# Head of a two-FFN transformer block: order by hand, tile by tile; rows without a slot made beside the experts; the sort moved behind the routing

## The chip, the cores and the metric

The kernel runs on one core of one Trainium2 chip. The metric is the device time of one execution in microseconds. Three runs of the kernel before took 4994.91 us (median), 4991.19 and 4998.73 us; a profiled execution, from which all rows below come, took 4992.54 us.

## The reference

Input x is 8 x 1024 tokens of 512 float32 values, T = 8192 tokens in all. Three steps follow one another, each on a layer norm LN without gain or offset:

```
x = x + 0.5 * FFN(LN(x));   x = x + Attention(LN(x));   x = x + 0.5 * FFN(LN(x))

FFN(h), E = 32 experts, C = 320 slots each, F = 512:
  probs = softmax(h @ w_router); top1 = argmax; gate = probs[top1]
  pos = place of the token among those of its expert, in token order
  accepted = pos < C
  y = (silu(g) * u) @ w_down,  g = h @ w_gate[top1],  u = h @ w_up[top1]
  return h + where(accepted, gate * y, 0)
```

The FFN returns h plus the expert's part, so each step adds x + h/2 to every token, and gate * y / 2 to those that got a slot. A token beyond the 320th of its expert has no slot and keeps x + h/2 alone. Attention has 16 heads of 32 and rotary tables. The same weights serve both FFNs.

## The kernel before

The work runs in four stages on one core: the head (routing for the first FFN), the first experts, the attention (which also routes for the second FFN), and the second experts.

**Head** (`tile_macaron`, L1215 to L1245). Eight groups of G = 8 tiles of 128 tokens. Each group is loaded in one DMA of 2 MB (L1231). Per tile, DVE takes mean and variance (`stats`, L113 and L114); per group, `normalizing` makes the scale: DVE adds epsilon (L124), POOL takes the power -0.5 (L125), DVE makes the shift `nmr` (L127) and the pair r2, n2 (L128, L129) for x + h/2. ACT writes h (`normalize`, L134), DVE writes x + h/2 in place (`rest`, L148), and the whole group goes to the DRAM array x1 (L1238). Per four tiles `logits` transposes h on PE (`tp`, L156), copies it on ACT (`xT`, L157), multiplies by the router (`pl`, L177), copies (`parts`, L182), folds (`lp`, L187) and copies (`lg`, L190). Per group `route` (L216 to L265) makes softmax and slots: mx, ex (exp on ACT, L219), one-hot `oh`, running counts `run`, two products on PE (`pp`, L234 and L238), position, and at last the integer `slot` (L265). Then POOL issues one indirect DMA per tile (L267), which writes each token's number and gate into the table at its slot. In this stage the framework's scheduler chooses the order of instructions.

**Experts** (`experts`, called once for each FFN). First the table is read back (`slots`, L378, on SP), DVE clears the two buffers `a` (L382), and `sorted` ranks the experts by their counts (L280 to L340), with its products in PSUM; DVE then copies part of the slots (L384), two products permute the slots (`pt`, L387), and POOL gathers the first experts' tokens (L454). SP loads each expert's three matrices (1 MB each, L445) as soon as the sorted `order` is there. `arm`, also from the sort, picks one of three code versions by the counts. The loop `feed` then runs 32 experts: products for gate and up (`gp`, `up`, L511), Silu on ACT (`sg`, L516), product on DVE (`a`, L534), transposes of the next expert (L499), down projection (`yp`, L547), the sum with x + h/2 (`ys`, L551), and one indirect DMA per 128 tokens (L565), which writes the finished rows. So in the first FFN the experts overwrite the rows of x1 of all tokens with a slot. Order on PE, ACT, DVE and POOL is as written; SP's queue is placed by the scheduler.

**Attention** (`Attention.run`) reads x1, works through heads by an order written out by hand, and in its last part routes for the second FFN in groups of four tiles (`finished`). Its end copies the counts, and `experts` starts again.

DMAs issued from SP go through one hardware queue in order; indirect DMAs are issued by POOL, one after another, in line with POOL's other instructions.

Of the kernel before, what the change touches and what calls it, by code (L numbers as in the profile page):

```python
# [22 lines left out]
P = 128  # L23
# [27 lines left out]
class Block:  # L51
# [64 lines left out]
    def normalizing(self, pool, mv):  # L116

        nc, G = self.nc, mv.shape[1]  # L120
        r, n, r2, n2 = (
            pool.tile([P, G], F32, tag=name, name=name) for name in ("rstd", "nmr", "r2", "n2")
        )
        nc.vector.tensor_scalar(r, mv[:, :, 1], EPS, None, ALU.add)  # L124
        nc.gpsimd.tensor_tensor(r, r, self.power[:, 0:G], ALU.pow)  # L125
        yield WAIT, 2
        nc.vector.scalar_tensor_tensor(n, mv[:, :, 0], -1.0, r, ALU.mult, ALU.mult)  # L127
        nc.vector.tensor_scalar(r2, r, 0.5, 1.0, ALU.mult, ALU.add)  # L128
        nc.vector.tensor_scalar(n2, n, 0.5, None, ALU.mult)  # L129
        return r, n, r2, n2  # L130
# [21 lines left out]
    def transposed(self, psum, tag, out, x):  # L152

        tp = psum.tile([P, self.KD, P], F32, tag=tag, name="tp")
        for k in range(self.KD):
            self.nc.tensor.transpose(tp[:, k, :], x[:, k * P : (k + 1) * P], self.ident)  # L156
        self.copy(out, tp)  # L157

    def logits(self, hs, lg, pool, psum, tag, bufs=2):

        nc, E, KD = self.nc, self.E, self.KD
        xT = pool.tile([P, KD, 4 * P], F32, tag="xT", bufs=bufs, name="xT")
        j = 0
        for h in hs:
            if isinstance(h, tuple):
                yield h
                continue
            yield PE, 0.6  # L170
            self.transposed(psum, tag, xT[:, :, j * P : (j + 1) * P], h)
            j += 1
        yield WAIT, 1
# [7 lines left out]
        parts = pool.tile([P, 4 * P], F32, tag="parts", bufs=1, name="parts")  # L181
# [11 lines left out]
    def route(self, t0, lg, pool, psum, tag, carry, table):  # L193
# [71 lines left out]
        nc.vector.tensor_scalar(slot, s, float(self.NS), None, ALU.add)  # L265
        for j in range(G):
            nc.gpsimd.indirect_dma_start(  # L267
                out=table[t0 + j],
                out_offset=bass.IndirectOffsetOnAxis(ap=slot[:, j : j + 1], axis=0),
                in_=row[:, j, :],  # L270
                in_offset=None,
            )
        return run[:, G, :]

    def sorted(self, pool, psum, counts, order, arm):
# [9 lines left out]
        pc = psum.tile([P, E], F32, tag="tp", name="pc")  # L285
        nc.tensor.matmul(pc, self.ones, counts, start=True, stop=True)
        pr = psum.tile([R, P], F32, tag="tp", name="pr")
# [3 lines left out]

        keys, mine = pool.tile([P, E], F32, name="keys"), pool.tile([R, E], F32, name="mine")
        nc.vector.scalar_tensor_tensor(keys, pc, float(E), self.rev[:, 0, :], ALU.mult, ALU.add)
        nc.vector.tensor_scalar(mine, pr[:, 0:E], float(E), None, ALU.mult)
# [26 lines left out]
        nc.vector.tensor_copy(cols[:, 1, :], pr[0:E, :])  # L321
        over, some = pool.tile([P, E], F32, name="over"), pool.tile([P, 2], F32, name="some")
        for i in range(2):
            pq = psum.tile([P, E], F32, tag="tp", name="pq")
# [15 lines left out]
        return matrix  # L340

    def experts(self, table, counts, src, dst, w_gate, w_up, w_down):
# [9 lines left out]
        views = dram_disjoint_views(dst, E * NB)  # L352
# [3 lines left out]
        with tc.tile_pool(name="et", bufs=1) as tp:  # L356
            R = NB * E
            order, come, go = (tp.tile([P, w], I32, name=name) for name, w in
                               (("order", E), ("come", R), ("go", R)))
            at = [tp.tile([P, R], F32, name=f"at{i}") for i in range(2)]  # L360
            ids, gates = at
            arm = tp.tile([P, 1], I32, name="arm")
# [9 lines left out]
            with (  # L372
# [8 lines left out]
                for t in acts:  # L381
                    nc.vector.memset(t, 0.0)  # L382
                matrix = self.sorted(fp, ps, counts, order, arm)
# [25 lines left out]
            for i in tc.Switch(which, len(self.profiles)):  # L409
                with (  # L410
# [5 lines left out]
                    expert = Expert(self, (wp, ap, ps), src, views, come, go, gates, acts)  # L416
# [10 lines left out]
class Expert:  # L427


    def __init__(self, s, pools, src, views, come, go, gates, acts):  # L430
        self.s, self.nc = s, s.nc
        self.wp, self.ap, self.ps = pools
        self.src, self.views = src, views
        self.come, self.go, self.gates, self.acts = come, go, gates, acts

        self.xs = 3 if self.wp is not self.ap else 2
# [11 lines left out]
    def gather(self, r, width):  # L448
# [11 lines left out]
        return SimpleNamespace(r=r, width=width, NB=NB, x=x)  # L460

# [57 lines left out]
    def feed(self, now, following, after):  # L519
# [5 lines left out]
        a, wd = self.acts[now.r % 2], now.weights[2]  # L525
        if following:
            self.measure(following)
        later = after and after()
        for f in range(KF):
# [5 lines left out]
            if following and f == 1:  # L535
                self.rests(following)
        if following:
# [34 lines left out]
class Attention:  # L572
# [13 lines left out]
    def __init__(  # L586
        self, s, L, B, x1, x2, out, table, inverse, zero, counts, weights, biases, cos, sin
# [3 lines left out]
        self.x1, self.x2, self.out, self.table, self.carry = x1, x2, out, table, zero  # L591
        self.inverse, self.counts = inverse, counts
# [121 lines left out]
    def run(self):  # L714
        nc, tc = self.nc, self.tc
        F, KD = mybir.EngineType, self.KD
        with (
# [6 lines left out]
            with tc.manual_schedule(engines={F.PE, F.Activation, F.DVE, F.Pool}):  # L724
# [29 lines left out]
                nc.vector.tensor_copy(self.counts, self.carry)  # L754
# [430 lines left out]
def tile_macaron(  # L1185
# [11 lines left out]
    x1 = dram.tile([T, D], F32, name="x1")  # L1197
# [9 lines left out]
    counts = const.tile([P, E], F32, name="counts")  # L1207
# [4 lines left out]

    with (
        tc.tile_pool(name="a", bufs=3) as pool,
        tc.tile_pool(name="aps", bufs=6, space=PSUM) as psum,  # L1215
    ):
        none = pool.tile([P, s.NS // P, 2], F32, tag="none", bufs=1, name="none")
        nc.vector.memset(none[:, :, 0], float(T))
        nc.vector.memset(none[:, :, 1], 0.0)
# [4 lines left out]
        views = dram_disjoint_views(tables[0], NT)  # L1224
        carry = zero
        for g in range(NG):
            rows = slice(g * G * P, (g + 1) * G * P)
            xg = pool.tile([P, G, D], F32, tag="xg", name="xg")
            hg = pool.tile([P, G, D], F32, tag="hg", name="hg")
            mv = pool.tile([P, G, 2], F32, tag="mv", name="mv")  # L1230
            nc.sync.dma_start(xg, xf[rows, :].rearrange("(j p) d -> p j d", p=P))  # L1231
            for j in range(G):
                s.stats(pool, mv[:, j, :], xg[:, j, :])
            by = at_once(s.normalizing(pool, mv))
            for j in range(G):
                s.normalize(hg[:, j, :], xg[:, j, :], by, j)
                s.rest(xg[:, j, :], xg[:, j, :], by, j)
            nc.sync.dma_start(x1[rows, :].rearrange("(j p) d -> p j d", p=P), xg)  # L1238
            lg = pool.tile([P, G, E], F32, tag="lg", name="lg")
            for j in range(0, G, 4):  # L1240
                at_once(s.logits(
                    [hg[:, j + i, :] for i in range(4)], lg[:, j : j + 4, :], pool, psum, "ps"
                ))
            carry = at_once(s.route(g * G, lg, pool, psum, "ps", carry, views))
        nc.vector.tensor_copy(counts, carry)  # L1245

    s.experts(tables[0], counts, xf, x1, w_gate, w_up, w_down)


    Attention(  # L1250
        s, L, B, x1, x2, of, dram_disjoint_views(tables[1], NT), inverse, zero, counts,
        (wqT, wkT, wvT, woT), (bq, bk, bv, bo), cos, sin,
    ).run()

    s.experts(tables[1], counts, x2, of, w_gate, w_up, w_down)
# [41 lines left out]
```

## Time and profile before

| Stage | us of the span |
|---|---|
| profiled execution (its own time) | 4992.54 |
| span of its instructions | 4990.8 |
| head: to the last slot | 197.2 |
| last table scatter issued (L267) | 206.37 |
| first product of the first expert (L511) | 240.53 |
| end of the last scatter of the first experts | 1055.5 |
| table read before the second experts (L378) | 4143.46 |
| first product of the second experts | 4174.70 |

A profile row reads: start, duration, engine, line, operation, out<-in, shapes, count, and in brackets the idle time of that engine before it with what ended it. PEld is PE's weight load. "issue" is time in which the engine waited for nothing that the profile shows. Of the span, PE is busy 4661.9 us (93%), DVE 2875.7, ACT 2887.6, POOL 723.8; DMA moves 485.93 MB. PEclk is the granted clock of PE as a share of full speed. Between 50 and 200 us it is 0.71 to 0.73; from 250 us on it is 1.00.

### The profile page before, as it was taken

To read this page: it belongs to the slowest core of one execution; us is meant where nothing else is said; L and a number is where in the kernel's file an instruction comes from. 1 tells how busy PE (TensorE), PEld (TensorE's weight loads), DVE (VectorE), ACT (ScalarE), POOL (GpSimd) and SP (SyncE) were. 2 spreads that over 40 slices of the span, in tenths; PEclk is the share of its full clock that TensorE was granted. 3 is DMA by queue.
4 is the path that set the end of the run, shared out by engine and by line. 5 is a ranking of instruction groups with operands and counts; after the bars stand their busy time and mean duration, and the time that the engine had idled before them with its cause. 6 is when DMAs were issued, how large, how long until landed. Compare 5 with 4: busy or idle time off the path is not lost.

```text
span 4990.8 us, 68660 instructions
## 1 busy us (share of the span) xinstructions
PE 4661.9 (93%) x24568; PEld 2144.3 (43%) x24568; DVE 2875.7 (58%) x5685; ACT 2887.6 (58%) x5794; POOL 723.8 (15%) x702
## 2 busy tenths in 40 slices
PE   4499999978899999999999999999999876999999
PEld 3366667742223333333333333333333224666677
DVE  6433333336766767777777777767766734333333
ACT  5311111107999888888888888888888831111111
POOL 2422222210000010110010110110110002222221
PEclk7699999988999999999999999999999987999999
DMA  6334445531111211212212212212211114445454
GB/s 226 138 126 165 161 167 175 197 110 28 43 27 40 80 50 54 72 46 61 68 45 64 69 41 66 69 41 64 60 42 58 52 65 147 153 162 170 161 194 137
DMA packets 284903, 485.93 MB, mean 97 GB/s; under 512 B 42248, under 2 KB 77522, under 8 KB 284544
## 3 DMA queue, kind: packets, MB, share of 16 engines
q1 hardware_dynamic: 254816, 404.35, 25.3%
q0 software_dynamic: 29440, 76.83, 4.9%
q8 instruction: 196, 3.21, 0.3%
q14 instruction: 163, 1.34, 0.1%
q10 hardware_dynamic: 288, 0.20, 0.0%
HBM read 363.34 MB, written 89.72 MB: 91 GB/s over the span
## 4 chain that ended last, share of the span: by engine, by line
PE 81%; DVE 8%; ACT 4%; issue 3%; POOL 1%; DMA 1%; SPq 1%; DVEq 0%; another core or an unknown queue 0%; ACTq 0%; POOLq 0%
PE sa L1022 13%; PE gp L511 9%; PE up L511 9%; PE pq L927 9%; PE po L1104 8%; PE yp L547 8%; PE sb L1002 5%; PE px L1130 4%; PE pv L972 4%; PE sb L1029 3%; ACT junk L1041 2%; DVE nm L1037 2%; PE tp L156 2%; PE tp L499 2%; PE yp L555 1%
## 5 line engine op out<-in xcount | busy, mean ns | idle before, releaser
L1037 DVE TENSOR_REDUCE nm<-sa 128x2 f32<-128x1024 f32 x1024 | 1249.2, 1221 | 649.9 <-PE sa L1022 391.6
L1041 ACT ACTIVATE junk<-sa,nm 128x512 f32<-128x512 f32 x2048 | 1408.2, 688 | 267.9 <-DVE nm L1037 195.2
L1022 PE MATMUL sa<-k,q 32*128 32x512 f32 x4096 | 1151.4, 646 | 19.6 <-ACT junk L1041 11.5
L1034 ACT ACTIVATE pr<-sb 128x1024 f32<-128x1024 f32 x1024 | 1041.4, 1019 | 101.6 <-PE sb L1029 95.5
L1029 PE MATMUL sb<-q,k 32*128 32x512 f32 x4096 | 1064.3, 603 | 0.0
L516 ACT ACTIVATE sg<-gp 128x320 f32<-128x320 f32 (+3 forms) x256 | 102.9, 402 | 1273.0 <-PE gp L511 973.0
L1104 PE MATMUL po<-pr,v 128*32 128x512 f32 x4096 | 550.1, 608 | 0.1
L511 PE MATMUL gp<-bT,wg 128*128 128x320 f32 (+3 forms) x2048 | 532.9, 403 | 2.6 <-DVE bT L502 2.6
L511 PE MATMUL up<-bT,wu 128*128 128x320 f32 (+3 forms) x2048 | 525.4, 399 | 0.0
L952 POOL TENSOR_TENSOR raw<-raw,cs 128x512 f32<-128x512 f32 x128 | 164.9, 1288 | 2471.9 <-DMA rot<-raw 1880.3
L927 PE MATMUL pq<-hT,wqk 128*128 128x512 f32 x1024 | 511.4, 624 | 7.3 <-DVE raw L942 3.7
L547 PE MATMUL yp<-wd,a 128*128 128x512 f32 x1024 | 453.7, 596 | 0.0
L511 PEld LDWEIGHTS gp<-bT,wg 128*128 128x128 f32 x2048 | 387.7, 191 | 118.7 <-issue 31.4
L1002 PE MATMUL sb<-mrow,ones 3*128 3x512 bf16 x2048 | 393.5, 385 | 45.0 <-ACT pr L1034 42.3
L534 DVE TENSOR_TENSOR a<-sg,up 128x320 f32<-128x320 f32 (+3 forms) x256 | 114.1, 446 | 548.6 <-PE up L511 531.6
L511 PEld LDWEIGHTS up<-bT,wu 128*128 128x128 f32 x2048 | 389.4, 190 | 94.6 <-issue 0.8
L1002 PEld LDWEIGHTS <-ones 3*128 3x128 bf16 x2048 | 100.6, 91 | 714.1 <-issue 672.4
L1041 ACT ACTIVATION_READ_ACCUMULATOR junk<-sa,nm 128x1 f32 x2048 | 397.9, 194 | 0.0
L1029 PEld LDWEIGHTS sb<-q,k 32*128 32x128 f32 x4096 | 360.4, 184 | 0.1
L1022 PEld LDWEIGHTS sa<-k,q 32*128 32x128 f32 x4096 | 305.2, 184 | 84.7 <-ACT pr L1034 34.5
L927 PEld LDWEIGHTS pq<-hT,wqk 128*128 128x128 f32 x1024 | 176.3, 191 | 326.0 <-issue 227.5
L551 DVE SCALAR_TENSOR_TENSOR ys<-yp,at,x 128x512 f32<-128x512 f32 x128 | 96.1, 750 | 369.0 <-PE yp L547 369.0
(175 smaller groups left out, 4213.1 us busy)
## 6 DMA issues: line engine op xcount, KB each, us to landing
wg<-in_w_gate SPq DMA_DIRECT2D x64, 1024.0 KB
wu<-in_w_up SPq DMA_DIRECT2D x64, 1024.0 KB
wd<-in_w_down SPq DMA_DIRECT2D x64, 1024.0 KB
rot<-raw SPq DMA_DIRECT2D x1024, 32.0 KB
xg<-in_x SPq DMA_DIRECT2D x8, 2048.0 KB
x<-xg SPq DMA_DIRECT2D x8, 2048.0 KB
xt<-x SPq DMA_DIRECT2D x64, 256.0 KB
xr<-x SPq DMA_DIRECT2D x64, 256.0 KB
```

The lines of the kernel that those rows point to most:

```text
L511: nc.tensor.matmul(acc, w[:, k, f * P : (f + 1) * P], to.bT[:, k, 0:width], start=(k == 0), stop=(k == s.KD - 1),)
L547: nc.tensor.matmul(yp, a[:, f, i * P : (i + 1) * P], wd[:, f, :], start=(f == 0), stop=(f == KF - 1),)
L927: nc.tensor.matmul(acc, w[:, which, k, :], self.hT[b, n][:, k, :], start=(k == 0), stop=(k == KD - 1),)
L972: nc.tensor.matmul(acc, hT[:, k, at : at + P], self.w_vo[:, k, :], start=(k == 0), stop=(k == KD - 1),)
L1002: nc.tensor.matmul(sb[:, h, :], self.ones16[at : at + 3, :], row[at : at + 3, :], start=True, stop=False,)
L1022: nc.tensor.matmul(sa[:, h, :], qa[at, (g * 4 + j) * P : (g * 4 + j + 1) * P], ka[at, m * 512 : (m + 1) * 512], start=True, stop=True,)
L1029: nc.tensor.matmul(sb[:, h, :], k[at, t * P : (t + 1) * P], q[at, n * 512 : (n + 1) * 512], start=False, stop=True,)
L1034: nc.scalar.activation(pr, sb, AF.Exp)
L1037: nc.vector.tensor_reduce(nm[:, m, j, pair : pair + 2], sa, AX.X, ALU.max, negate=True)
L1041: nc.scalar.activation(self.junk, sa[:, h - pair, :], AF.Exp, bias=nm[:, m, j, h : h + 1], accum_out=se[:, m, j, h : h + 1],)
L1104: nc.tensor.matmul(self.po[at : at + HD, :], self.v[b][t][:, c * P + at : c * P + at + HD], prs[h // 2 * 2][:, h % 2, :], start=(t == 0), ...
L1130: nc.tensor.matmul(acc, self.oT[b, c, half][:, j * P : (j + 1) * P], self.w_vo[:, c, :], start=False, stop=(c == KD - 1),)
```

## The change

Four things are done.

1. The head is written out by hand (`front`) for PE, ACT, DVE and POOL. It goes tile by tile: in each step, h of one tile on ACT, its transposes on PE, the copy of the tile before (seven of eight on ACT, every eighth on DVE), the stats of the tile ten ahead on DVE, and one step of each piece of other work at hand: a group's scale, the router products of four tiles, a route. Groups are 4, then seven times 8, then 4 tiles. Loads are 1 MB (four tiles).
2. x + h/2 isn't made in the head any more, and x1 isn't written there. The scale and shift of all tokens stay in SBUF (`rest`), and `route` also makes `spare`: for a token without a slot its own number, else T.
3. In the first experts' loop, expert r loads two tiles of x, ACT makes x + h/2 of them, and POOL scatters them by `spare`; rows whose index is T fall outside the bounds and are skipped. x1 becomes a DRAM tensor of its own name.
4. `sorted` runs right behind the routing, at the end of the head and at the end of the attention, in a pool of its own; the result is handed to `experts`. The buffers `a` are cleared by POOL.

```diff
-    def normalizing(self, pool, mv):
+    def normalizing(self, pool, mv, to=None):
...
-        r, n, r2, n2 = (
+        r, n, r2, n2 = to or (
...
+        if spare is not None:
+            nc.vector.tensor_scalar(ok, pos, float(C), None, ALU.is_ge)
+            nc.vector.scalar_tensor_tensor(u, token, float(-self.T), ok, ALU.add, ALU.mult)
+            nc.vector.tensor_scalar(spare[:, t0 : t0 + G], u, float(self.T), None, ALU.add)
         for j in range(G):
             nc.gpsimd.indirect_dma_start(
...
+    def front(self, pool, psum, x, rest, spare, carry, table):
...
+        def routed(g):
+
+            while state.next < g:
+                yield
+            state.carry = yield from self.route(
+                starts[g], lgs[g], pool, psum, "lp", state.carry, table, spare
+            )
+            state.next += 1
+
+        def products(t):
+            g = group[t]
+            lg, at = lgs[g], t // 4 * 4 - starts[g]
+            yield from self.routers(
+                xTs.pop(t // 4), lg[:, at : at + 4, :], pool, psum, "lp", bufs=2
+            )
+            if t + 1 == starts[g] + sizes[g]:
+                work.append(routed(g))
...
+        ahead, late = G + 2, None
+        load(0)
+        load(4)
+        for i in range(-ahead, NT + 2):
+            if 0 <= i < NT:
+                g = group[i]
+                if i == starts[g]:
+                    lgs[g] = pool.tile([P, sizes[g], E], F32, tag="lg", bufs=3, name="lg")
+                h = pool.tile([P, D], F32, tag="h", bufs=4, name="h")
+                self.normalize(h, tile_of(i), (r, n, None, None), i)
+                if i % 4 == 0:
+                    xTs[i // 4] = pool.tile([P, KD, 4 * P], F32, tag="xT", bufs=3, name="xT")
+                tp = self.turned(psum, "tp", h)
+            if late:
+                to, from_, j = late
+                (nc.vector.tensor_copy if j % G == G - 1 else nc.scalar.copy)(to, from_)
+                if j % 4 == 3:
+                    work.append(products(j))
+            late = None
+            if 0 <= i < NT:
+                late = xTs[i // 4][:, :, i % 4 * P : (i % 4 + 1) * P], tp, i
+            t = i + ahead
+            if t < NT:
+                if t % 4 == 0 and t + G < NT:
+                    load(t + G)
+                self.stats(pool, mv[:, t, :], tile_of(t))
+                if t + 1 == starts[group[t]] + sizes[group[t]]:
+                    work.insert(0, scaled(group[t]))
+            advance()
+        while work:
+            advance()
+        return state.carry
...
-        pr = psum.tile([R, P], F32, tag="tp", name="pr")
+        nc.vector.scalar_tensor_tensor(keys, pc, float(E), self.rev[:, 0, :], ALU.mult, ALU.add)
+        pr = psum.tile([R, P], F32, tag=tag, name="pr")
...
+        nc.vector.tensor_copy(many, pr)
+        nc.vector.tensor_scalar(mine, many[:, 0:E], float(E), None, ALU.mult)
...
                 for t in acts:
-                    nc.vector.memset(t, 0.0)
-                matrix = self.sorted(fp, ps, counts, order, arm)
+                    nc.gpsimd.memset(t, 0.0)
...
+    def fetch_others(self, r):
+
+        s = self.s
+        n = s.NT // s.E
+        x = self.ap.tile([P, n, s.D], F32, tag="all", name="all")
+        self.nc.sync.dma_start(
+            x, self.src[r * n * P : (r + 1) * n * P, :].rearrange("(j p) d -> p j d", p=P)
+        )
+        return x
+
+    def put_others(self, r, x):
+
+        s, (scale, shift, spare) = self.s, self.others
+        n = s.NT // s.E
+        for j in range(n):
+            t = r * n + j
+            self.nc.scalar.activation(
+                x[:, j, :], x[:, j, :], AF.Identity, bias=shift[:, t : t + 1],
+                scale=scale[:, t : t + 1],
+            )
+            self.nc.gpsimd.indirect_dma_start(
+                out=self.views[s.E * s.NB + t],
+                out_offset=bass.IndirectOffsetOnAxis(ap=spare[:, t : t + 1], axis=0),
+                in_=x[:, j, :], in_offset=None, bounds_check=s.T - 1, oob_is_err=False,
+            )
...
         a, wd = self.acts[now.r % 2], now.weights[2]
+        others = self.fetch_others(now.r) if self.others else None
         if following:
             self.measure(following)
...
+        if others:
+            self.put_others(now.r, others)
         if following:
             self.transpose(following)
...
-                nc.vector.tensor_copy(self.counts, self.carry)
+                self.ranks = self.s.sorted(self.ranking, psum, "m", self.carry)
...
-        for g in range(NG):
...
-            for j in range(G):
-                s.normalize(hg[:, j, :], xg[:, j, :], by, j)
-                s.rest(xg[:, j, :], xg[:, j, :], by, j)
-            nc.sync.dma_start(x1[rows, :].rearrange("(j p) d -> p j d", p=P), xg)
...
+        counts = s.front(
+            pool, psum, xf, rest, spare, zero, dram_disjoint_views(tables[0], NT)
+        )
+        ranks = s.sorted(ranking, psum, "lp", counts)
```

A generator advances by one `yield` in each step of the loop, whatever the yield says: in the head the kinds and sizes that `normalizing`, `routers` and `route` yield are not weighed.

## The prediction

> **What bounds the kernel now.** I read the page first (the slices), then the busy time by stretches, the timeline of the head, and the chain of waits from 160 to 262 us. Line numbers are those of the profile.
>
> ```profile
> span 4990.8 us, 68660 instructions
> PE   4499999978899999999999999999999876999999
> DVE  6433333336766767777777777767766734333333
> POOL 2422222210000010110010110110110002222221
> PEclk7699999988999999999999999999999987999999
> ```
>
> PE is full from the third slice on; only the first two slices (the head) and the two dips near slices 9 and 33 are not PE's. The change touches the head, the first expert loop and the second dip.
>
> ```profile
> 50.00:100.00 50.00, 28.19 (x151) 19.88 (x152) 34.65 (x137) 23.57 (x44) 19.00 (x18) 0.72 0.73 213
> 240.50:300.00 59.50, 59.35 (x212) 36.49 (x214) 20.20 (x49) 9.12 (x15) 11.84 (x13) 0.95 0.37 130
> ```
>
> Columns: stretch, then busy us of PE, PE loads, DVE, ACT, POOL, then granted clock, DMA share, GB/s. In the head no engine is full: engines wait for one another. From 240.5 on PE has 59.35 of 59.5, so there the rest is hidden. The head's waits show best here:
>
> ```profile
> 54.40 0.15 DVE L265 TENSOR_SCALAR slot<-s 128x8 int32<-128x8 f32 x1
> 54.86 1.17 POOL L267 DMA_INDIRECT table<-row,slot  x1 [16.19 <-DVE slot L265]
> ...
> 63.92 0.96 POOL L267 DMA_INDIRECT table<-row,slot  x1 [0.30 <-issue]
> 64.91 1.67 POOL L125 TENSOR_TENSOR rstd<-rstd,power 128x8 f32<-128x8 f32 x1
> 66.61 0.17 DVE L127 SCALAR_TENSOR_TENSOR nmr<-mv,rstd 128x8 f32<-128x8 f32 x1 [5.74 <-POOL rstd L125]
> ...
> 66.82 0.81 ACT L134 ACTIVATE hg<-xg,nmr,rstd 128x512 f32<-128x512 f32 x1 [7.91 <-DVE nmr L127]
> ```
>
> POOL gives out eight scatters one by one, 1.265 us apart, and the power that the next group's scale needs stands behind them: DVE idles 5.74 us, ACT 7.91. This befell two of the eight groups (scatters at 54.86 and 101.60); elsewhere the power ran before the scatters or found POOL free.
>
> ```profile
> 206.37 0.96 POOL L267 DMA_INDIRECT table<-row,slot  x1 [0.30 <-issue]
> 208.73 0.34 SPq L378 DMA_DIRECT2D slots<-table  x1
> 209.18 1.12 DVE L382 MEMSET a<- 128x1280 f32 x1 [11.94 <-DMA table<-row,slot]
> 219.13 0.22 DVE L384 COPY slots<-slots 32x128 f32<-32x128 f32 x1
> 222.13 0.98 POOL L454 DMA_INDIRECT x<-in_x,come  x1 [14.80 <-DVE go L395]
> 240.53 4.60 PE L511 MATMUL gp<-bT,wg 128*128 128x320 f32 x8 [1.41 <-DVE bT L502]
> ```
>
> The way out of the head: last scatter, table read back, two memsets and the sort on DVE (209.18 to 219.13), gather, first expert. The same before the second experts:
>
> ```profile
> 4143.46 0.33 SPq L378 DMA_DIRECT2D slots<-table  x1
> ...
> 4153.45 0.22 DVE L384 COPY slots<-slots 32x128 f32<-32x128 f32 x1
> ```
>
> **The second experts' start.** The sort is moved behind the routing and the memsets to POOL; the read of the table no longer finds the sort in front. Sort: 4145.89 to 4153.42, 7.5 us, plus 0.2 for the added copy and about 1 for its products sharing one PSUM buffer; it starts at 4136.3 behind the slots and ends near 4145. The read, issued at 4143.46, has no landing of its own in the trace: between 1.65 us (`rot<-raw`, 1110.13) and 4.36 (`bias`, 1056.63 to its reader at 1060.99, on a busy queue); I take 2.1, as the scatters land (206.37, 2.09). So the copy of the slots runs at 4145.6 in place of 4153.45: **-7.5 us**, between -5.5 and -8. What hides the sort is four scatters and their landing (4136.61 to 4142.89) and the read; without that cover 7.5 come back. The memsets on POOL cost, by its 128x128 one of 0.208 and 128x1 of 0.10, from 1.2 (slope) to 2.1 us (in proportion) each, so POOL is free by 4147.1 at the latest and the gather is due at 4148.5. SP loads weights about 8 us earlier, but as long before the gather as now (4 us), so the two collide as today.
>
> **The head.** Gone: 64 `rest` operations of DVE (34.9 us) and 16.8 MB of writes. They lie on today's chain in part (`xg` L148 is 2.4% of the chain up to 600 us, 14 us), but the new order makes a chain of its own, so I walk that; the changed kernel as built shows it on each in-order queue. Per eight tiles, DVE: slot, spare, stats, rstd+eps, stats, **nmr**, then one route interleaved with six stats, slot. POOL: eight scatters, then the power for that nmr. ACT: per tile h and the copy of the tile before; two `parts`, two `lg`, one exp. PE: transposes, `pl`, `lp`, `pp` in line with them.
>
> I time it from one group's slot to the next (a cycle).
>
> *Slot to nmr.* The scatters are released at slot and the power comes right behind them: 54.55 (end of slot) to 66.61 = **12.0 us** in the row above; in its place DVE has 2.4 us of work (0.6 spare, two stats at 0.81 as at 358.37 to 359.99, rstd 0.2). Queued behind nmr on DVE are the stats, the next route and every eighth copy of `xT`; ACT stops at the exp that needs this route's `ex`, and PE then runs out of tiles. So all three are late, not DVE alone. Groups 4 to 7 meet it in full; group 3 stands behind four scatters: 0.3 + 4.86 (4106.21 to 4111.07) + 1.7 = 6.85. Groups 0 to 2 and 8 don't.
>
> *Nmr to slot.* Stats, mx, ex to 2.0 (0.31 + 0.81 + 0.45 + 0.46); exp 0.42, h 0.75, to 3.2; PE, idle since ACT stopped, transposes and runs `lp` at half clock (1.06, 1.92 as at 28.59) to 6.1; `lg`, h, copy, h to 8.45; transposes 1.06, `pp` 2.3, `pl` 1.94 cold, or 0.55, 1.5, 1.06 warm; `parts` 0.6, h 0.75, transposes, `xT` on DVE 0.7, stats 0.8, ten small steps 2.07 (195.17 to 197.24). All cold 19.8, all warm 16.1. Which clock is granted here no row shows; 25.94 to 33.96 stayed cold with hardly a gap, while 174.16 was warm by 177.3. I take **18.0**. The Trainium skill, "TensorE: Matmul & The Clock Gate", "Part 1: The HAM clock gate", speaks against such an order: about 3.4 us idle halves the clock and 3.4 us busy restores it. An estimate by that page alone is 17.2 for the walk and 4 us less for the whole; the row at 30.31 (x16 in 3.65, against 1.94 at 162.35) shows the full clock later than that.
>
> *Start.* The first load is 1 MB, not 2 MB: at 388 GB/s (6 to 10.5 us) 2.7 less than 10.58, so 7.8. Thirteen stats 10.5, `fold` 0.8, two waits for the power 2.4: 21.5. Twelve tiles to the `xT` of tile 15 at 2.15 us (ACT's own 11.9 per eight, four waits of 1.0 for PE, 1.5 for `pp`: 17.5 warm; 21 cold): 47.3; +2.9: first slot at 50.2 (55.6 cold); now it is at 54.55.
>
> *Sum.* Slots: 50.2; +6.85 + 18 = 75; three cycles of 30: 165; +12 + 17.2 (few stats left) = 194.3; one cycle without the block, 18: 212.3. Routes 7 and 8 follow in 9.5 and 7.2 us (188.33 to 197.25 and 4099.32 to 4105.91, and 0.6 for spare), sooner than POOL's 10.1 per group of eight, so POOL runs the last 20 scatters in a row: the last starts at 212.6 + 19 x 1.265 = 236.6, against 206.37 now. From there: 2.36 to the read, 2.1 landing, 21.4 as now (219.13 to 240.53): first expert at 262.5 in place of 240.53, **+22 us**. The same sum with 16.1 throughout gives +12 (all warm), with 19.8 and a first slot at 55.6 +39 (all cold). The sort, about 9 us from the last route's slots (229), is over before the read lands at 241, and the memsets (239 to 243 at the latest) before the gather at 244, so both cost nothing here either; SP's queue holds nothing in front of the read but loads long issued.
>
> **The expert loop.** Per expert two ACT operations (0.74 each, 1.5), two scatters (2.5 on POOL), 512 KB on SP. Cover: ACT idles 15.28 us there before its next `sg`, POOL 16.40 before the `ys` scatter; the load is issued some 20 us ahead at 150 to 170 GB/s of 390 seen. Zero; if ACT's were uncovered, 32 x 1.5 = 47. Nearly all of those scatters' rows fall outside the bounds; whether they write none or all, PE doesn't wait for them.
>
> **Sum:** +22 - 7.5 = +14.5 on the profiled 4992.5 us (span 4990.8 and 1.7 around it); the median of the runs, 4994.9, lies 2.4 above, so **5010 us**, its own range 5003 to 5018.
>
> **Rivals.** *PE warm throughout*: +12 - 7.5 = +4.5, 4999. For it: clock 0.72 in this stage now. Against: idle stretches of some 8 us in each cycle. *Cold throughout*: +39 - 7.5, 5026; the transposes near 1090, one tile at a time, ran at clock 0.50. *POOL's scatters don't hold the power up* (the other side): then cycles of 17.6: slot 6 at 50.2 + 6 x 17.6 = 156, last scatter 180, first expert 206, -34.5 - 7.5: 4953. Its place is POOL's queue, 36 scatters in front of a power that DVE waits for; it decides once a scatter costs POOL under 0.85 us (break-even, 14.5/36 off 1.265), and passes -10 us under 0.6. For it: six groups escaped it now. Against: the order is now fixed, and 54.86 to 66.61. *The added rows aren't hidden*: +47, 5057; against it the idle times just given.
>
> **How the numbers follow.** Forecast 0.52, warm 0.21, cold 0.14, no block 0.08, uncovered 0.05. A measurement can tell about 0.2% (10 us) from no change: faster 0.08; slower 0.14 + 0.05 + 0.46 of the forecast; same 0.21 + 0.06. From 4990 to 5029 leaves out the last two and some tails, 0.2 together.
>
> **What would show it.** Right: nmr behind power by 9 us of idle DVE in groups 4 to 7, slots 30 us apart, 20 scatters in a row at the end, the first `gp` near 262; the slots copy 2 us behind the read in both places; PE unbroken in the experts. Wrong: powers ahead of scatters, slots under 20 us apart, or gaps before `gp` in the loop.

## The result, and the profile after

| | median us | runs |
|---|---|---|
| before | 4994.91 | 4991.19 to 4998.84 (5 runs) |
| after | 5020.19 | 5019.37 to 5024.05 (5 runs) |

The ratio is 1.0051, with a 95% interval of 1.0037 to 1.0066: 25.3 us slower, where the forecast was 15 us (5010). That is 2 us above the forecast's own range (5003 to 5018) and inside the whole range (4990 to 5029). The profiled execution took 5020.19 us, its span is 5018.3; against the span before (4990.8) that is +27.5.

The page of the kernel after, its span and slices:

```profile
span 5018.3 us, 68972 instructions
PE   5489999978899999999999999999999876999998
PEclk6689999988999999999999999999999997999999
```

PE is full from the fourth slice on, as it was from the third before: a slice is 125 us, and the head has grown by a quarter of one. The busy time by stretches, with columns as before:

```profile
50.00:100.00 50.00, 29.73 (x124) 19.98 (x124) 27.01 (x104) 20.32 (x37) 15.16 (x14) 0.57 0.29 85
274.50:334.00 59.50, 59.31 (x216) 36.42 (x216) 19.83 (x49) 11.93 (x19) 16.21 (x17) 0.96 0.49 166
```

In the head DVE does less (27.01 in place of 34.65 us in 50), the DMA moves less data (85 GB/s, not 213), and still no engine is full; PE's clock is down from 0.72 to 0.57. In the experts PE has 59.31 of 59.5 us, as before: the added loads (166 GB/s, not 130), ACT and POOL work is covered.

The timeline of one cycle of the new head, group 4's scale behind group 1's scatters:

```profile
77.17 0.17 DVE L273 TENSOR_SCALAR slot<-s 128x8 int32<-128x8 f32 x1
77.63 1.03 POOL L279 DMA_INDIRECT table<-row,slot  x1 [17.78 <-DVE u L276]
...
86.56 0.96 POOL L279 DMA_INDIRECT table<-row,slot  x1 [0.30 <-issue]
87.54 1.67 POOL L125 TENSOR_TENSOR rstd<-rstd,power 128x8 f32<-128x8 f32 x1
89.25 0.17 DVE L127 SCALAR_TENSOR_TENSOR nmr<-mv,rstd 128x8 f32<-128x8 f32 x1 [9.59 <-POOL rstd L125]
```

Eight scatters, then the power, then `nmr`, with DVE idle for 9.59 us. It comes again at 119.28, 149.32 and 178.39 (9.58 to 9.59 each) and, behind four scatters, at 59.89 (4.67): 43 us of idle DVE. The way out of the head, and the place before the second experts:

```profile
241.47 0.96 POOL L279 DMA_INDIRECT table<-row,slot  x1 [0.31 <-issue]
243.53 0.71 PE L390 MATMUL pr<-ones,wide 128*96 128x128 f32 x2 [12.69 <-remote]
...
245.54 0.35 SPq L478 DMA_DIRECT2D slots<-table  x1
...
253.13 0.22 DVE L483 COPY slots<-slots 32x128 f32<-32x128 f32 x1 [0.25 <-issue]
...
4174.02 0.33 SPq L478 DMA_DIRECT2D slots<-table  x1
...
4176.03 0.60 DVE L483 COPY slots<-slots 32x128 f32<-32x128 f32 x1 [0.83 <-DMA slots<-table]
```

In the second place the copy of the slots follows the read by 2.0 us, as forecast. In the head it follows by 7.6: the sort, whose second product is `pr` at 243.53, was still at its beginning when the last scatter went out, and the copy stands behind it on DVE. The stages side by side, all from the two timelines:

| Stage | before | after | difference |
|---|---|---|---|
| start to last table scatter of the head | 206.37 | 241.47 | +35.1 |
| from it to the first `gp` | 34.16 | 33.10 | -1.1 |
| to the last scatter of the first experts | 812.20 | 811.72 | -0.5 |
| to the last table scatter of the attention | 3087.75 | 3084.75 | -3.0 |
| from it to the second experts' first `gp` | 34.22 | 25.49 | -8.7 |
| to the last scatter of the second experts | 811.19 | 811.72 | +0.5 |
| from it to the end of the span | 4.91 | 10.05 | +5.1 |

The differences add up to 27.5. The attention's -3.0 is no effect: a second profile of the kernel before (r4 below) has 3084.44 for that stage. The same profile has 209.33 for the first row and 243.76 for the first `gp`, 3 us later than here, so the head's growth is known to some 3 us (31 to 34).

### The profile page after: what moved, and what is told of

The parts are those of the page before. It is cut to its first block, busy times and chain, and to the rows that moved or that the text cites. A ratio compares the mean times of both kernels' runs of the same rounds, so it can differ in the third digit from the quotient of the medians.

```text
span 5018.3 us, 68972 instructions
## 1 busy us (share of the span) xinstructions
PE 4682.0 (93%) x24572; PEld 2150.1 (43%) x24572; DVE 2869.2 (57%) x5678; ACT 2927.2 (58%) x5851; POOL 790.2 (16%) x773
## 4 chain that ended last, share of the span: by engine, by line
PE 80%; DVE 8%; ACT 5%; issue 3%; POOL 1%; DMA 1%; SPq 1%; DVEq 0%; POOLq 0%; ACTq 0%
PE sa L1153 13%; PE gp L638 9%; PE up L638 9%; PE pq L1058 8%; PE yp L677 8%; PE po L1235 8%; PE sb L1133 5%; PE px L1261 4%; PE pv L1103 4%; PE sb L1160 3%; ACT junk L1172 2%; DVE nm L1168 2%; PE tp L156 2%; PE tp L626 2%; PE yp L685 1%
```

## Experiments

The experiments ran in four sets, each on one chip beside the kernel before; the chips are called A to D. The kernel before had medians of 4992.56 (A), 4985.97 (B), 4993.85 (C) and 4985.52 us (D), so ratios are compared across chips, and microseconds within one. The expectations for e6 to e9 give ranges in microseconds that start from runs on A; the kernel before is 6.6 us faster on B, where these four then ran.

### The power ahead of the scatters

`e1_power_first` (chip A) lets the scatters of a group wait for one step of the loop, so that POOL's list has the power first:

```diff
-        for j in range(G):
-            nc.gpsimd.indirect_dma_start(
+        def scatters():
+            yield
+            for j in range(G):
+                nc.gpsimd.indirect_dma_start(
...
+        if later is None:
+            list(scatters())
+        else:
+            later.append(scatters())
...
-                starts[g], lgs[g], pool, psum, "lp", state.carry, table, spare
+                starts[g], lgs[g], pool, psum, "lp", state.carry, table, spare, work
```

> After the change, with one edit: the eight table scatters of a group are issued one step later, so that on POOL the power of the next group to be normalised stands ahead of them and not behind them. Nothing else on any engine's list changes. My theory (POOL's queue holds the power back behind eight scatters): DVE's stalls ahead of nmr in the head (4.67 and then 9.6 us in each of four groups, 43 us in all) go, the cycle of a group falls from 30.0 to 20 to 21 us, the first gp starts 43 us sooner, at about 231 instead of 274.57, and the kernel takes 4977 (4970 to 4985), less than before the change. Rival, a slow TensorE clock or the chain of the products bounds the head: the stall turns into another wait of the same length, the cycle stays at 28 to 30 and the time within 6 us of 5020. Second question, the last routing chain and the sort, which ran 10 us slower in the head than in the second place: if scatters on POOL beside DVE's small operations do that, it is still there or longer, since 28 scatters now run back to back; if it belongs to something else, it may be gone, and then the gain is nearer 50.

Measured: 4980.87 us, ratio 0.9977 (0.9968 to 0.9986). Its timeline, one cycle:

```profile
74.87 0.17 DVE L273 TENSOR_SCALAR slot<-s 128x8 int32<-128x8 f32 x1
76.62 1.67 POOL L125 TENSOR_TENSOR rstd<-rstd,power 128x8 f32<-128x8 f32 x1 [14.42 <-DVE rstd L124]
78.33 0.17 DVE L127 SCALAR_TENSOR_TENSOR nmr<-mv,rstd 128x8 f32<-128x8 f32 x1 [0.98 <-POOL rstd L125]
78.49 1.03 POOL L281 DMA_INDIRECT table<-row,slot  x1 [0.20 <-issue]
...
95.56 0.17 DVE L273 TENSOR_SCALAR slot<-s 128x8 int32<-128x8 f32 x1
```

`nmr` now waits 0.98 us for the power, the scatters go out behind it beside the next group's work, and slot follows slot by 20.7 us and not 30.0. The last scatter is at 201.43 in place of 241.47, 40.0 us sooner, and the first `gp` at 233.83 in place of 274.57, 40.7 us sooner (43 expected). `r1_after` and `r2_power_first` below repeat the pair on one chip: 5020.92 and 4985.58 us. So the block costs 35 to 40 us and is what made the change slower. PE's clock rose with it, from 0.59 to 0.69 in 55 to 110 us: the low clock was a companion of the stall, and the rival that saw the clock as the bound falls.

### The second part of the change, and what in it pays

`e3_sort_back` (chip A) is the kernel after with the sort inside the experts' stage again; `e5_before_sort` (A) is the kernel before with the sort alone moved; `e9_before_sort_pool` (chip B) adds to it the memsets on POOL.

e3, against the kernel after:

```diff
+                matrix, order, arm = self.sorted(ranking, ps, "tp", counts)
                 nc.vector.tensor_copy(rows[R - E : R, n:P, :], rows[R - E : R, 0:n, :])
...
-                self.ranks = self.s.sorted(self.ranking, psum, "m", self.carry)
+                nc.vector.tensor_copy(self.counts, self.carry)
```

e5, against the kernel before:

```diff
-                matrix = self.sorted(fp, ps, counts, order, arm)
...
-        nc.vector.tensor_copy(counts, carry)
+        ranks = s.sorted(ranking, psum, "ps", carry)
```

e9, against e5:

```diff
-                    nc.vector.memset(t, 0.0)
+                    nc.gpsimd.memset(t, 0.0)
```

> After the change, with the sort put back: the counts are copied, and the sort runs inside the experts' stage behind the issue of the table's read, as before the change. The new head and the new rows stay. The traces say that the moved sort is worth 8.7 us in the second place (last scatter to first gp 34.22 before, 25.49 after) and only 1.1 in the head (34.16 and 33.1). If that is the whole of it: 5020 + 10 = 5030 (5026 to 5034), and the last scatter to gp near 34 in both places. Rival, the sort ahead of the read is what delays the head's read and gather: then the head gets shorter without it, the last routing chain and the read run as in the second place, and the time is 5020 + 8.7 - 6 = 5023 or less.

> Before the change, with the sort alone moved: it runs right behind the last group's routing, in both places, beside the last scatters; the head, x + h/2 and the experts' loop stay as before the change. My forecast priced this part at 7.5 us in the second place and nothing in the head. With what the trace after shows (8.7 in the second place): head undisturbed, the sort (8.5 us) lies beside the last eight scatters and goes off the path, about 7 us: 4995 - 16 = 4979 (4975 to 4984). If the sort beside scatters is slowed as it was in the head after the change (12 us late): 4995 - 10 = 4985 (4982 to 4990). If the sort moved is worth nothing: 4995.

> Before the change, with the sort right behind the routing and the two memsets of a on POOL: the whole of the change's second part, with the old head and the old rows. Without the memsets on POOL the last scatter stood 27.4 us ahead of the second gp; with them on POOL (after the change, and with the sort put back) 25.4 to 25.5. Theory, the memsets on DVE, which wait for the scatters to land, held up what stood behind them: 2 us less in the second place, about 1 in the head, 4978.6 - 3 = 4975.6 (4973 to 4979). Rival, the memsets on POOL stand ahead of the gathers and hold them up: 4979 to 4982. POOL's drain at the end: 3.8 us if the memsets on POOL have no part in its 9.0 us after the change.

| kernel | sort | memsets | last scatter to `gp`, second place | ratio |
|---|---|---|---|---|
| before | in the stage | DVE | 34.22 | 1 |
| e5 | behind the routing | DVE | 27.43 | 0.9973 (0.9964 to 0.9982) |
| e9 | behind the routing | POOL | 26.38 | 0.9966 (0.9952 to 0.9979) |
| e3 | in the stage | POOL | 25.40 | 1.0056 (1.0043 to 1.0070) |
| after | behind the routing | POOL | 25.49 | 1.0051 (1.0037 to 1.0066) |

e5 and e9 came out as expected (4978.63 and 4969.07 us): e5 is 13.9 us under the kernel before of its chip and e9 16.9, where 3 more were expected, though the two intervals overlap. Of the 2 us expected of the memsets in the second place 1.05 came (27.43 to 26.38). e3 did not come out as expected: putting the sort back cost the second place nothing. Its time, 5021.39 us, is the one that its rival named, but not for the rival's reason: the head did not get shorter, from its last scatter to the first `gp` it takes 36.24 us against 33.10 of the kernel after. What held the sort up is seen in the kernel before, second place:

```profile
4143.50 1.12 DVE L382 MEMSET a<- 128x1280 f32 x1 [7.11 <-DMA table<-row,slot]
4144.84 1.12 DVE L382 MEMSET a<- 128x1280 f32 x1 [0.22 <-issue]
4145.89 0.28 DVE L283 COPY wide<-counts 128x32 f32<-128x32 f32 x3
```

The memsets wait until the scatters have landed (7.11 us), and the sort, which needs nothing from the table, stands behind them on DVE. In e3:

```profile
4178.10 2.27 POOL L481 MEMSET a<- 128x1280 f32 x2 [2.04 <-DVE over L433]
...
4179.06 0.15 DVE L440 CAST arm<-both 128x1 int32<-128x1 f32 x1
...
4179.82 0.63 DVE L483 COPY slots<-slots 32x128 f32<-32x128 f32 x1 [0.61 <-DMA slots<-table]
```

With the memsets on POOL the sort runs beside the scatters from where it stood, and ends at 4179.06, before the read lands. So the gain of 8.7 us in the second place is mostly that of one wait: the memsets' move takes all of it away (e3), the sort's move alone 6.8 us (e5), and there the sort's move is worth nothing beside the memsets'. In the head of these kernels it was worth 3.1 us (33.10 against 36.24, one profile each), less than the spread of the two times. With the old head the second part also pays there: from the last scatter to the first `gp` e5 takes 26.38 us and e9 25.49, the kernel before 34.16.

e9, the old head and the second part alone, has the lowest ratio, but its interval overlaps those of e5 and e1, so which is the fastest isn't settled. The profiles of e9 and of e6 below, both on chip B, show what the new head is worth with the power first and nothing late: the first `gp` at 226.83 in place of 234.92, 8.1 us, of which the longer end of the program (the drain, below) takes 5.9 back.

### The late operations at the end of the head

In the head of the kernel after, the last group's slots and the sort ran late. The same lines of that kernel, first in the second place, then in the head:

```profile
4165.92 0.17 DVE L269 TENSOR_SCALAR s<-s 128x4 f32<-128x4 f32 x1
4166.12 0.16 DVE L270 TENSOR_TENSOR s<-s,token 128x4 f32<-128x4 f32 x1
...
4168.38 0.18 DVE L394 TENSOR_SCALAR mine<-many 96x32 f32<-96x32 f32 x1
```

```profile
232.92 0.17 DVE L269 TENSOR_SCALAR s<-s 128x4 f32<-128x4 f32 x1
233.56 0.16 DVE L270 TENSOR_TENSOR s<-s,token 128x4 f32<-128x4 f32 x1 [0.47 <-DVE s L269]
...
236.40 0.22 DVE L273 TENSOR_SCALAR slot<-s 128x4 int32<-128x4 f32 x1 [1.23 <-DVE s L272]
...
239.07 0.18 DVE L388 SCALAR_TENSOR_TENSOR keys<-pc,rev 128x32 f32<-128x32 f32 x1
...
244.40 2.27 POOL L482 MEMSET a<- 128x1280 f32 x2 [1.96 <-remote]
245.52 1.19 DVE L394 TENSOR_SCALAR mine<-many 96x32 f32<-96x32 f32 x1 [0.95 <-DVE many L393]
```

From the start of `s` (L269) to that of `mine` (L394) it is 2.5 us there, 12.6 here. Operations that wait for another one's end start 0.5 to 4.3 us after it (`pr`, shown above at 243.53, 4.3 us after the end of `keys`). It stops at about 245.5, when the scatters have landed and SP issues the read. That `mine` then takes 1.19 us and not 0.18 is something else: POOL's two memsets run from 244.40 to 246.67, and `mine` ends at 246.71. Three tests of one idea, that the length of POOL's unbroken train of scatters (20 here) does it, all built on e1. e6 gives out eight scatters more, into a scratch table:

```diff
+            if t0 == 36:
+                later.append(scatters(self.scratch))
```

e7 leaves out the seventh group's eight scatters, and with them the experts' part of that group's tokens in the result:

```diff
-            nc.vector.tensor_scalar(ok, pos, float(C), None, ALU.is_ge)
+            nc.vector.tensor_scalar(ok, pos, float(C) if t0 != 44 else -1.0, None, ALU.is_ge)
...
-        else:
+        elif t0 != 44:
             later.append(scatters())
```

e8 puts a gap behind the seventh group's:

```diff
+            if later is not None and t0 == 44:
+                junk = pool.tile([P, 1280], F32, tag="junk", bufs=1, name="junk")
+                nc.gpsimd.memset(junk, 0.0)
+                nc.gpsimd.memset(junk, 0.0)
```

> The kernel with the power first, and eight more scatters: the sixth group's rows are written once more, into a scratch table that nobody reads, while POOL would be idle (166.9 to 177.0). POOL then runs 36 scatters back to back from 156.7 on instead of 28 in two trains. Theory, the length of the train: in three kernels the first late operation on DVE comes 12.6 to 12.8 scatters after the start of the unbroken train (217.16 to 233.1, 177.15 to 193.3, 217.98 to 234.1), so here late operations start at about 173 to 175 instead of 193.3, the routing chains of the last three groups are slow too, and the first gp starts 5 to 15 us later than 233.83, the kernel at 4986 to 4996. Rival, the place in the program (the last group's routing and the sort, whatever POOL does): first late operation at 193 as it was, first gp and time within 2 us of 233.83 and 4980.9. Beside that, POOL's drain at the end (9.0 us with the new head and rows, 3.8 without): if it grows with the number of indirect transfers, 64 more of which went with 5.2 us, it grows by 0.7 here.

> The kernel with the power first, and eight scatters fewer: the seventh group's rows get no slot, so their experts' part is left out, and they are written as rows without a slot. The last train is 12 scatters (from about 187) instead of 20 and ends at the same time; the counts, and with them the work of the experts, stay. Theory, the length of the train: no late operations or hardly any, the sort takes some 9.6 us from the last group's s on (192.9) as in the second place and is over at 202 to 204 instead of 212, the table's read is issued at 203 to 205 instead of 205.4, the gathers start at 208 to 210 instead of 214.9, the first gp at 227 to 229 instead of 233.8, and the kernel takes 4974 to 4977. Rival, the place in the program: the sort ends at 212, gp at 233 to 234, the kernel at 4980.9.

> The kernel with the power first, and a gap in the train: two memsets of an unused tile (2.3 us on POOL) stand between the seventh group's scatters and the twelve after them, so that the train is 8, a gap, and 12. Theory, the length of the unbroken train: the gap starts the count again, late operations go, the last scatter starts 2.3 us later (203.7), but the sort is over by 204, the gathers start at about 210.5 instead of 214.9, the kernel takes 4975 to 4978. Rival, POOL's total of scatters in flight (a short gap changes nothing) or the place in the program: the late operations stay, the last scatter is 2.3 us later, the kernel takes 4981 to 4984.

On chip B none of the three showed a late operation, e6 with its 36 scatters as little as the others:

```profile
193.19 0.32 DVE L397 SCALAR_TENSOR_TENSOR keys<-pc,rev 128x32 f32<-128x32 f32 x1
...
193.65 0.71 PE L399 MATMUL pr<-ones,wide 128*96 128x128 f32 x2 [4.14 <-DVE keys L397]
```

`pr` starts 0.14 us after the end of `keys`, where it was 4.3 in the kernel after, and the first `gp` comes at 226.83. The times are 4972.72, 4969.71 and 4976.44 us, the ratios 0.9974, 0.9968 and 0.9981. By itself e6 refutes the idea. But e1 had not run on that chip, so four kernels were run once more, unchanged, on one chip (C), and later the gap again (D).

> The kernel after the change once more, unchanged, together with three others on one chip. The late operations at the end of the head were there in three kernels profiled on one chip (first late operation 12.7 scatters into the last train), and not in three profiled on another, one of which has a longer train; that was the length of the train against the place in the program, and neither can be the whole of it. Theory, the execution or the chip decides, not the kernel: here they may be missing from this kernel too, and then the sort is over before the read lands and the first gp comes about 27 us after the last scatter starts instead of 33.1. Rival, the kernel decides: the last scatter to gp is 33 again. The time against before: 1.004 to 1.006 in either case with the block in place.

> The kernel with the power first, unchanged, on the same chip as its variants. By the first theory (execution or chip) the last scatter to the first gp is 26 to 27 us if the late operations are missing, 32.4 if they are there, whatever they are in the others; by the kernel theory 32.4. The time: 0.997 to 0.998 of before.

> The kernel with eight scatters more, unchanged, on the same chip. If the late operations belong to the kernel, none here; if to the chip or the execution, they can be here while they are missing from others, or all alike. POOL's drain at the end: 9.67 again, if it follows the number of indirect transfers.

> The kernel before the change, profiled on the same chip as the three others, so that their stages stand side by side. Expected from its first profile: first gp at 240.5, first experts 812, last scatter to second gp 34.2, POOL's drain 3.8; ratio 1.000 within 0.2%.

> The kernel with the power first and the gap in the train, once more, to meet a chip on which trains of scatters make operations late (two chips of three so far: there 20 scatters in a train made the first operation late after 12.7 of them, and 28 in a longer train cost another 13 us; on the third chip neither did). With trains of 8 and 12 the theory of the train's length expects no late operations on either kind of chip: pr within 0.5 us of keys, the sort over before the read lands, last scatter to gp 26 to 27 us, and a time of 0.995 to 0.998 of before. If what counts is the number of scatters in some 25 us and not an unbroken train, the gap of 2.3 us changes little: last scatter to gp 31 to 33 and 0.998 to 0.9995. On a chip of the third kind nothing is learnt but the time.

| kernel, chip | longest last train | late at the end of the head | last scatter to first `gp` | us | ratio to before |
|---|---|---|---|---|---|
| after | 20 | yes | 33.10 | 5020.19 | 1.0051 |
| r1 (after), C | 20 | yes | 32.77 | 5020.92 | 1.0055 (1.0038 to 1.0072) |
| e1, A | 20 | yes | 32.40 | 4980.87 | 0.9977 |
| r2 (e1), C | 20 | yes | 33.17 | 4985.58 | 0.9985 (0.9975 to 0.9994) |
| r3 (e6), C | 16, then 20 | yes | 33.23 | 4993.41 | 0.9997 (0.9988 to 1.0007) |
| e6, B | 36 | no | 26.68 | 4972.72 | 0.9974 (0.9965 to 0.9983) |
| e7, B | 12 | no | 27.05 | 4969.71 | 0.9968 (0.9954 to 0.9981) |
| e8, B | 8, gap, 12 | no | 27.33 | 4976.44 | 0.9981 (0.9972 to 0.9990) |
| r5 (e8), D | 8, gap, 12 | no | 27.07 | 4974.74 | 0.9977 (0.9967 to 0.9987) |
| e5, A | 8 | no | 26.38 | 4978.63 | 0.9973 |

r4, the kernel before again, gave 4996.12 us, 1.0004 (0.9995 to 1.0014), with its first `gp` at 243.76 where 240.5 was expected. On chip C the longer train is late twice, the first time well before the place where the other kernels are:

```profile
178.49 1.06 PE L246 MATMUL pp<-run,ones 128*128 128x256 f32 x2
...
185.80 0.42 DVE L250 TENSOR_TENSOR lg<-pp,oh 128x256 f32<-128x256 f32 x1 [17.34 <-remote]
185.89 0.58 ACT L189 COPY parts<-pl 128x512 f32<-128x512 f32 x1 [6.55 <-remote]
```

The product ends at 179.55, and its reader starts 6.3 us later; the train began at 163.10, thirteen scatters earlier, and its last scatter ended at 183.07. The first `gp` comes at 249.08, 12.9 us after r2's, as e6's theory had it (5 to 15), and the kernel is 7.8 us slower. So the place in the program is not the cause: a longer train brings late operations where there were none. In these kernels they begin at about the thirteenth scatter of a train, on two of four chips (A and C, besides the run of the result), and up to 36 in a row did nothing on B. e3, also on A, had it too. Thirteen is no threshold, though. Beside the old head's trains of eight, single copies of `lg` on ACT start late as well: at 82.13, 1.8 us after the end of `lp`, in the kernel before; at 85.02 and 173.42, 2.1 and 1.9 us after it, in r4 (C); at 85.54, 2.0 us after it, in e5 (A); none by more than 0.4 us in e9 (B). Whether that is the same effect was not tested. What remains open is why, and why one chip and not another: both runs of the gap met chips on which nothing may be late anyway (on B e6 shows it; on D only the gap ran), so whether the gap would help on A or C isn't known. Nor was e9 run there; its trains, like e5's, follow the old head's eight per group.

### POOL's drain at the end

The last row of the table of stages was in no forecast. POOL ends the program with a drain; the longest of its three durations (ns, the last of min/median/max) in the kernels before, after, e6 and e7:

```profile
L1293 POOLq DRAIN  x3: 40/115/3812, 4986.1 to 4990.5; - x3
```

```profile
L1413 POOLq DRAIN  x3: 40/115/9017, 5008.5 to 5018.1; - x3
```

```profile
L1424 POOLq DRAIN  x3: 40/115/9672, 4953.6 to 4963.8; - x3
```

```profile
L1420 POOLq DRAIN  x3: 40/115/8364, 4958.7 to 4967.7; - x3
```

The change adds 64 indirect transfers (the rows without a slot) and 5.2 us of drain: 81 ns each. e6 has eight more than that, +0.655 us; e7 eight fewer, -0.653: 82 ns each. The line doesn't go through zero: the kernel before has 460 indirect transfers and a drain of 3.8 us, where 81 ns each would be 37. So the price is known for what was added to those 460, and not for the first ones. The expectation for e6 said 0.7. e5 and e9, without those transfers, stay at 3.8.

## Why the prediction was right, and where it was off

**The block on POOL: right.** From the end of slot to `nmr` 12.0 us were forecast; it took 11.9 (77.34 to 89.25). From `nmr` to the end of the next slot 18.0 were forecast, between all warm and all cold; it took 18.1 (89.25 to 107.38). That this is so close is partly luck: 18.0 was a choice between the two bounds, and which clock would be granted wasn't known. It was 0.50 up to 101 us, 1.00 from 102 to 105, and 0.59 over the whole stretch. The estimate by the Trainium skill, "TensorE: Matmul & The Clock Gate", "Part 1: The HAM clock gate", was 17.2; the measurement lies nearer to the walk by rows. The cycle of 30 came three times within 1 us (30.0, 30.0, 29.1). e1 shows it from the other side.

**The slots: 2.7 us late at the start, 4.6 at the end.** The first was forecast for 50.2 and ended at 52.9. The cycles made up more than half of that (the sixth slot's end: 195.5, forecast 194.3); then the one cycle without the block, put at 18, took 21.4. So the last scatter came at 241.47, not 236.6: +4.9.

**The sort beside the scatters in the head: the step that failed.** It was to be over by 241 and cost nothing; it was over at 252.9. From the last scatter to `gp` 25.9 us were forecast and 33.1 taken, +7.2: the read was issued 4.1 us after the last scatter and not 2.4, and the copy of the slots, behind the sort on DVE, came 7.6 us after the read and not 2.1. The order was as forecast; the durations weren't, because of the late operations, and because the late sort then met POOL's memsets, which were put at nothing too (1.0 us at `mine`). Without late operations the same stretch is 26.7 to 27.3 (e6, e7, e8, r5). Together with the slots the head cost +34.0 and not +22.

**The second place: right in size, half right in cause.** -8.7 for -7.5, just beyond the bounds of -5.5 and -8. I put it down to the sort's place; e3 shows that the memsets' move alone does all of it, e5 that the sort's alone does 6.8.

**The experts' loop: right.** -0.5 and +0.5 us around 812. The rival "uncovered" (+47) falls by the traces alone; the added work was not varied by itself.

**The end: a missing term.** 64 transfers were priced at their issue beside PE, and at nothing after it; they lengthen the drain by 5.2 (3.8 to 9.0).

**The sum.** +34.04 (head) - 8.73 (second place) + 5.14 (end) - 2.95 (the three stages between, which vary by as much from run to run) is +27.5 on the profile, where +14.5 was forecast. The block held as the mechanism; the slots' size (+4.9), the sort's cover in the head (+7.2) and the drain (+5.1), less what the second place and the three stages gave, make the difference. The rivals "warm" and "cold" were distances in one cycle whose time turned out at the middle between them, and "no block" was never near.

## What to carry to other kernels

In an order written by hand, look at what each in-order queue holds ahead of a short operation that another engine waits for: here one step's delay of eight scatters was worth 35 to 40 us, more than the whole of the change had won elsewhere. When a step is moved and time is saved, undo each half: the wait that went away may belong to its neighbour (here two memsets). Work that hides in a loop can still be paid for at the end, and a saving that rests on small operations beside a long train of transfers should be measured on more than one chip.

## What the runs showed of the hardware that I had not expected

- In long trains of indirect transfers on POOL, from about the thirteenth on, operations of DVE, ACT and PE that wait for another engine or for their own last result started 0.5 to 6.3 us late, until about when the transfers had landed (kernel after, e1, e3, r1, r2, r3); on two chips of four besides the run of the result, and not on B, which was given 36 in a row (e6). Single copies on ACT were 1.8 to 2.1 us late beside trains of eight as well.
- Each indirect transfer that POOL issued beyond the 460 of the kernel before added 81 to 82 ns to POOL's drain at the end of the program, in the head or in the experts' loop (56, 64 and 72 more: 8.364, 9.017 and 9.672 us, from 3.812).
- A memset of 128x1280 takes POOL 1.17 us, about as long as DVE (1.12); but DVE's copy of the slots (32x128, float32 from SBUF to SBUF) beside it takes 0.52 to 0.85 us in place of 0.22, and ends 0.07 to 0.08 us after the memsets do (after: 4176.63 behind 4176.55; e3: 4180.45 behind 4180.37). The Trainium skill, "SBUF — State Buffer", "Terms", calls the pair of ports that DVE and GpSimd share exclusive, and the loser blocked in full for the length of the instruction; the rows agree for this copy and for `mine` in the head (246.71 behind 246.67). Not every operation of DVE is held: a reduction at 4174.31 (0.19 us), also beside the memsets, is not slowed.
- The kernel before itself differs by 8 us between the chips A to D (4985.5 to 4993.9). Late operations were seen on the two slower ones (A 4992.56, C 4993.85) and not on the two faster (B 4985.97, D 4985.52, there with the gap alone); four chips don't show that one has to do with the other.
